# A four-layer hybrid kernel: the image stored once, the first block's sums fetched in two transfers, preparation ahead of the feed-forward

## The chip, the cores and the metric

One Trainium2 chip, one core. The kernel is one launch on that core. The metric is device time in microseconds (us): the time from launch to end of the program as the device measures it, lower is better. It is given as the median of several runs. A separate execution was recorded by the hardware profiler. Engines are named as in the profile: PE is the matrix engine (PEld its weight loads), DVE the vector engine, ACT the scalar (activation) engine, POOL the general engine, SP the engine that issues the transfers (DMA).

## The reference

The input `x` is four images of 128 channels and 64 by 64 pixels, fp32. Each of four layers normalizes and adds to a residual stream. Cut to what matters here:

```python
# layer 0, for each image (x already group-normalized, called xa)
feat = gelu(dwconv3x3(xa, conv1_w) + conv1_b)
ca   = sigmoid(relu(feat.mean((2, 3)) @ ca1_w.T) @ ca2_w.T)
feat = gelu(dwconv3x3(feat * ca, conv2_w) + conv2_b)
sm   = mean over 4x4 patches of 0.7 * sigmoid(head(feat)) + 0.3 * sigmoid(10 * var(xa over channels))
idx  = argsort(-sm)                     # 256 patches; ties keep the lower index first
... the pixels in that order go through a selective scan (Mamba), and back; x += result
x = x + conv3x3(_gn(x)) + bias          # layer 1
# layer 2: t has 4096 tokens of 128 features for each of the 4 images; n = _ln_t(t)
q    = qz_ring(n as 16 heads of 8 + rx_theta)          # queries, keys and values are the same q
attn = softmax(q q^T / sqrt(8));  ctx = attn q         # 4096 x 4096 per head
x1   = ln(n + ctx @ w_comb.T + b_comb) * g1 + beta1    # the first residual
zf   = cos(x1[:8]) * cos(ry_theta)
t    = t + ln(x1 + relu(zf @ w1.T + b1) @ w2.T + b2) * g2 + beta2
t    = t + expert_ffn(ln(t))
# layer 3: linear attention, then another expert_ffn
```

## The kernel before, in words

Data lie channel-major, 128 channels on 128 partitions, and tokens along the free dimension, in chunks of 512 (8 chunks per image, `NCH`).

**Layers 0 and 1** (`layers01`). For each image `in_order(b)` computes the patch order and the reordered tokens, and `scan` runs the selective scan over them. `in_order(0)` runs alone at the start. After that, while image b is scanned, `in_order(b + 1)` is interleaved with it one turn at a time; in the last scan the ends of the images take its place. Inside a scan the order of all five engines is the program's order (a schedule written by hand, SP included): what is issued first runs first on its engine, and a waiting instruction holds those behind it.

In `in_order`, the group-normalized image is filled chunk by chunk into `xp`, padded to 66 by 66. Each depthwise 3x3 convolution runs on PE from a tile `under` of 96 partitions: three row shifts (ky) of 32 channels, for four groups of channels. To build it, `stored(img, i, half)` (L443) writes the image to DRAM three times, once for each ky, with 12 transfers for each half, into `image_d[i]`, and `gather(i, c)` (L453) reads one chunk back with one transfer of 792 KB. Image 0 is `xp`; its first half is stored at the seventh fill and its second after the border of `fp` is set. `first` convolves and its gelu (ACT, L130) writes `fp`, which is image 1, stored in halves once chunks 4 and 7 are there (`first_stored`). After the channel attention, `second` convolves from image 1. A gather is issued three turns ahead of its convolution. `sort` then ranks the 256 patch scores; for the ties it makes a mask `before` (L581) for each half on DVE.

In the scan, for each chunk and group ACT makes `decay` (L907), DVE runs the recurrence `hs` (L911), POOL multiplies by the C factors (L915) and PE sums (`y_ps`).

**Layer 2** (`layer2_attention`), for the blocks b = 0 to 3, one image each: first a transition, in which `prepare(b)` and the tail of the block before, `feed_forward(b - 1)`, run side by side; then `attention(b)`.

- `prepare(b)` has six stages for each of the 8 chunks: fetch, centred, norm, products, running, store. Then it loads the keys and queries of the first head (L1210, 32 transfers) and rounds them on POOL (L1218).
- `attention(b)` goes head by head: PE makes the scores, ACT the exponentials `ex` (L1534), and PE the weighted values: by columns into `ctx` (stored as `num_d` and `den_d`, L1473 and L1474) and, through DVE's 32x32 transposes and the tile `turned_v`, by rows into `acc`. Only half of the symmetric score matrix is computed; the sums of the first quarter of the tokens arrive from both sides, and their second part is stored for each head by L1436 into `around_d`. The values `v` of the next pair of heads are loaded at L1338.
- `feed_forward(b)` has nine stages: fetch, divisors, attended, first_centred, first_norm, cosines, hidden, last_centred, last_norm. Its chunk order is 2 to 7, then 0 and 1. A generator beside it, `firsts`, calls `gathered(c)` for chunks 0 and 1, which need the stored second part: 16 transfers for each chunk (L1582), one for each head, then sums on POOL (L1589, L1594). `divisors` transposes and adds the two halves of the denominators by four products with the constant `pick`, and `rc` (L1610) spreads the reciprocals over the features. `last_norm` adds to x on POOL (L1666) and stores x (L1667).

A transition's generators are run by `run` in round robin, one step of each per round, in the order in which they stand in `parts`. In a transition the engines' order is chosen by a planner which gives priority to what stands earlier in the program; in `attention` it is written by hand for PE, DVE and POOL. The tiles of the transition and those of `attention` use the same memory one after the other, so the first tiles of `attention` wait for the last ones of the transition.

`layernorm_steps` is the normalization with an affine part that is used by both: PE sums the given terms into `ln_xc` (L91; products with `K.center` remove the mean over features, and weights such as `w_comb` are centred once at setup), ACT squares it (`ln_sq`, L107) and copies it (`ln_kept`, L109), PE sums the squares, and DVE and POOL scale (L118 to L126).

**Then** come the experts' layer, layer 3 and the experts' layer again, which the change doesn't touch.

Of the kernel before, what the change touches and what calls it, by code (L numbers as in the profile page):

```python
# [17 lines left out]
P = 128  # L18
NB = 4
HW = 64  # L20
# [10 lines left out]
class Common:  # L31
# [67 lines left out]
    def layernorm_steps(self, out, terms, work, psum, affine=None, bufs=2):  # L99
# [7 lines left out]
        nc.scalar.activation(sq, xc, AF.Square, bias=shift)  # L107
        kept = work.tile([P, CH], F32, name="ln_kept", bufs=bufs)
        nc.scalar.activation(kept, xc, AF.Identity, bias=shift)  # L109
# [160 lines left out]
def layers01(K, xd, dpool, w, w1):  # L270
# [9 lines left out]
    with ExitStack() as ctx:  # L280
# [44 lines left out]
        image_d = [dpool.tile([4, 96, HW * (HW + 2)], F32, name=f"image_d{i}") for i in range(2)]  # L325
# [52 lines left out]
        ones256 = K.ones[:, 0:1].to_broadcast([P, 256])  # L378

# [43 lines left out]
        def in_order(b, made, work, psum):  # L423
# [13 lines left out]
            def stored(img, i, half):  # L437


                n = HW // 2 * (HW + 2)  # L440
                for g in range(4):
                    for ky in range(3):
                        nc.sync.dma_start(  # L443
                            out=image_d[i][g, 32 * ky : 32 * ky + 32, n * half : n * half + n],
                            in_=img[32 * g : 32 * g + 32, HW // 2 * half + ky : HW // 2 * (half + 1) + ky, :].rearrange(
                                "p y x -> p (y x)"
                            ),
                        )

            def gather(i, c):  # L450
                n = 8 * (HW + 2)
                t = unders[c] = work.tile([96, 4, n], F32, name="under", bufs=2)
                nc.sync.dma_start(out=t, in_=image_d[i][:, :, n * c : n * c + n].rearrange("g q f -> q g f"))  # L453
# [31 lines left out]
            for c in range(NCH):  # L485
                fill(c)
                if c == 6:
                    stored(xp, 0, 0)
                yield
# [6 lines left out]
            stored(xp, 0, 1)  # L496

            def first_stored(c):
                if c in (4, 7):
                    stored(fp, 1, c // 5)  # L500
# [66 lines left out]
            def sort():  # L567
# [6 lines left out]
                for h in range(2):  # L574
# [5 lines left out]
                    before = small.tile([P, 256], F32, name="before")  # L580
                    nc.vector.scalar_tensor_tensor(before, K.col, K.row[:, h : h + 1], ones256, ALU.is_gt, ALU.mult)  # L581
                    eq = small.tile([P, 256], F32, name="eq", tag="rank_eq")
                    nc.vector.scalar_tensor_tensor(eq, sm, cl, before, ALU.is_equal, ALU.mult)
# [520 lines left out]
def layer2_attention(K, xd, dpool, w):  # L1104
# [6 lines left out]
    with ExitStack() as ctx:  # L1111
# [48 lines left out]
        pick = cst.tile([2 * NH, NH], F32, name="pick")  # L1160
        nc.vector.tensor_tensor(pick, K.ident[0 : 2 * NH, 0:NH], K.ident[0 : 2 * NH, NH : 2 * NH], ALU.add)
# [22 lines left out]
        around_d = dpool.tile([NH, P, L // NJ // 4], F32, name="around_d")  # L1184
# [135 lines left out]
        def attention(qt, first, dsum, big, two, work, pssc, psctx, psacc):  # L1320
# [83 lines left out]
            def turn():  # L1404
# [28 lines left out]
                if i == 0:  # L1433


                    nc.sync.dma_start(out=around_d[h], in_=accs[h][:, 0].rearrange("p t r -> p (t r)"))  # L1436
# [121 lines left out]
        def feed_forward(b, dsum, work, psum):  # L1558
# [17 lines left out]
            def gathered(c):  # L1576
# [4 lines left out]
                for h in range(NH):  # L1581
                    nc.sync.dma_start(  # L1582
                        out=part[HD * h : HD * h + HD],
                        in_=around_d[h, :, c * P : (c + 1) * P].rearrange("(n d) f -> d n f", d=HD),
                    )
                    if h % 4 == 3:
                        yield
                yield
# [32 lines left out]
            def first_centred(c):  # L1621
# [3 lines left out]
                    x1, [(w_comb, num[:, 0]), (K.center, nrm)], work, psum, (b_comb, g1, beta1), bufs=3  # L1625
# [507 lines left out]
```

## Time and profile before

| what | us |
|---|---|
| median of 3 runs | 10019.67 (10018.24 to 10020.51) |
| the profiled execution | 10014.33, span 10012.5 |
| PE busy | 8755.8 (87%), mean granted clock 0.916 |
| ACT busy | 7414.1 (74%) |
| DVE busy | 7222.2 (72%) |
| POOL busy | 4804.1 (48%) |

| stretch of the span | us |
|---|---|
| front: image 0 alone | 0 to about 280 |
| scans 0, 1, 2 with the next image's order | to about 880, 1480, 2105 |
| scan 3 with the ends of the images | to 2850 |
| `prepare(0)` | 2850 to 2977 |
| attention 0, and the transition after it | 2977.1 to 4258.2, to 4466.6 |
| attention 1, and the transition after it | 4466.6 to 5753.6, to 5962.0 |
| attention 2, and the transition after it | 5962.0 to 7248.8, to 7457.0 |
| attention 3, and the last feed-forward | 7457.0 to 8743.9, to 8887.7 |
| experts, layer 3, experts | 8888 to 10012.5 |

How to read the profile: it is one execution. A row of a table of groups names the line, the engine, the operation, the tile written and the tiles read, the shape, the count, the busy time and the mean duration, and then the idle time of the engine just before these instructions with what ended it. A line can be that of a helper (L91 is the helper that issues the products). A waits line says which instruction stood idle, and for which one it waited. The chain of waits follows back, from the last instruction, what each step was released by. In a table of stretches each engine's busy time is given with its count of instructions, then the granted clock of PE, the mean busy share of the 16 DMA engines and the rate.

### The profile page before, as it was taken

Reading aid. Unit: us, or ns where it says so; the run is one execution under the profiler, and the core shown is the slowest. Engines: PE = TensorE matmul, PEld = TensorE weight load, DVE = VectorE, ACT = ScalarE, POOL = GpSimd, SP = SyncE. Lnnn points to the kernel's source line nnn. Section 1 sums busy time; section 2 is a strip of 40 time slices with the busy share of each in tenths; the row PEclk is TensorE's granted clock in tenths of the full one; section 3 lists DMA queues with packets and bytes.
Section 4 is the critical chain, followed back from the end, with each engine's and each line's share of the span. In section 5 each row is a group of like instructions: output and inputs, shape, how many; then the busy total and the mean of one; then the engine's idle time right before and its main releaser. Section 6 shows DMA issues by size and latency. Waiting matters only on the chain.

```text
span 10012.5 us, 187862 instructions
## 1 busy us (share of the span) xinstructions
PE 8755.8 (87%) x74074; PEld 3353.2 (33%) x74074; DVE 7222.2 (72%) x7883; ACT 7414.1 (74%) x10669; POOL 4804.1 (48%) x3175
## 2 busy tenths in 40 slices
PE   5687888889859999979999979999979999967767
PEld 1122222235433333333333333333333333323433
DVE  1779797998738888848888858888758888743463
ACT  2666766654439999969999969999969999941531
POOL 0567586775525555545555545555545555420000
PEclk9787887889979999989999989999989999978888
DMA  5634536222221211141211141211141111133004
GB/s 127 150 88 101 134 79 152 69 73 81 74 70 37 41 39 39 30 115 38 39 39 39 29 115 39 39 38 39 29 115 39 38 39 39 33 100 118 2 18 152
DMA packets 578291, 669.38 MB, mean 67 GB/s; under 512 B 113592, under 2 KB 369664, under 8 KB 570240
## 3 DMA queue, kind: packets, MB, share of 16 engines
q1 hardware_dynamic: 577408, 657.36, 27.1%
q8 instruction: 584, 9.57, 0.4%
q14 instruction: 299, 2.45, 0.1%
HBM read 446.84 MB, written 143.13 MB: 59 GB/s over the span
## 4 chain that ended last, share of the span: by engine, by line
PE 45%; DVE 4%; DMA 2%; ACT 2%; POOL 1%; issue 1%; SPq 1%; DVEq 0%; POOLq 0%; ACTq 0%
PE ctx_ps L91 20%; PE acc_ps L91 10%; PE score L91 8%; PE ln_xc L91 1%; DMA w<-in_L_ffn_weight 1%; PE ln_var L91 1%; PE hid_ps L91 1%; PE kv L91 1%; PE tok_t L1829 0%; PE ln_var L121 0%; PE pool L91 0%; PE ans_ps L91 0%; DVE ctx L1468 0%; PE o_ps L91 0%; SPq L1210 0%
## 5 line engine op out<-in xcount | busy, mean ns | idle before, releaser
L1534 ACT ACTIVATE ex<-score 128x1024 f32<-128x1024 f32 x5120 | 4927.9, 1037 | 176.0 <-PE score L91 90.2
L91 PE MATMUL ctx_ps<-ex,qt 128*32 128x512 f32 x20480 | 2736.5, 606 | 19.8 <-DVE ctx L1468 19.8
L1483 POOL TENSOR_TENSOR folded<-ex 128x1024 f32<-128x1024 f32 x512 | 1224.2, 2391 | 2124.0 <-ACT ex L1534 1866.1
L1540 DVE STREAM_TRANSPOSE turned<-ex 128x1024 f32<-128x1024 f32 x1536 | 1885.9, 1228 | 351.5 <-ACT ex L1534 279.1
L1516 DVE STREAM_TRANSPOSE turned<-ex 128x1024 f32<-128x1024 f32 x1532 | 1843.0, 1203 | 0.0
L91 PE MATMUL acc_ps<-turned,turned_v 128*32 128x256 f32 x24576 | 1769.4, 379 | 3.0 <-DVE turned L1546 3.0
L911 DVE TENSOR_TENSOR_SCAN hs<-decay,carry,hs 128x512 f32<-128x512 f32 x1024 | 1245.8, 1266 | 248.2 <-ACT decay L907 234.9
L91 PE MATMUL score<-queries,keys 32*128 32x512 f32 x10240 | 1333.6, 497 | 64.4 <-POOL queries L1218 35.8
L91 PEld LDWEIGHTS acc_ps<-turned,turned_v 128*32 128x32 f32 x24576 | 800.8, 110 | 1476.5 <-issue 1327.2
L915 POOL TENSOR_TENSOR hs<-hs,c_sb 128x1024 f32<-128x1024 f32 x512 | 1207.5, 2358 | 108.9 <-DMA c_sb<-c_d 66.5
L907 ACT ACTIVATE decay<-dt,a_neg 128x512 f32<-128x512 f32 x1024 | 693.0, 689 | 662.5 <-DVE hs L911 653.0
L91 PEld LDWEIGHTS score<-queries,keys 32*128 32x128 f32 x10240 | 512.1, 182 | 1160.4 <-ACT ex L1534 801.8
L1346 POOL TENSOR_TENSOR turned_v<-v,quarter 128x1024 f32<-128x1024 f32 x256 | 612.5, 2393 | 266.3 <-PE acc_ps L91 221.8
L91 PE MATMUL y_ps<-hs,pair 128*64 128x512 f32 x2048 | 664.0, 776 | 27.0 <-POOL hs L915 26.9
L1484 POOL TENSOR_TENSOR quarters<-folded 128x512 f32<-128x512 f32 x512 | 658.0, 1285 | 40.1
L91 PEld LDWEIGHTS ctx_ps<-ex,qt 128*32 128x32 f32 x20480 | 406.5, 108 | 655.4 <-issue 599.3
L900 DVE TENSOR_TENSOR hs<-dtx,b_ps 128x2048 f32<-128x2048 f32 x256 | 580.5, 2267 | 55.1 <-PE b_ps L91 29.8
L91 PE MATMUL b_ps<-dbc,state 32*64 32x512 f32 x1024 | 339.6, 745 | 224.5 <-DVE hs L900 224.4
L1534 ACT ACTIVATION_READ_ACCUMULATOR ex<-score 128x1 f32 x2048 | 437.7, 214 | 0.0
L914 POOL COPY carry<-hs 128x2 f32<-128x2 f32 x512 | 98.1, 192 | 700.1 <-DVE hs L911 673.9
L1468 DVE COPY ctx<-ctx_ps 128x512 f32<-128x512 f32 x256 | 176.9, 691 | 329.2 <-PE ctx_ps L91 323.5
L91 PE MATMUL conv<-under,deep 96*32 96x512 f32 x1536 | 217.9, 708 | 136.6 <-DMA under<-image_d 128.3
(371 smaller groups left out, 9156.9 us busy)
## 6 DMA issues: line engine op xcount, KB each, us to landing
c_sb<-c_d SPq DMA_DIRECT2D x512, 128.0 KB
queries<-head_d SPq DMA_DIRECT2D x1024, 64.0 KB
keys<-head_d SPq DMA_DIRECT2D x1024, 64.0 KB
under<-image_d SPq DMA_DIRECT2D x64, 792.0 KB
dt<-dt SPq DMA_DIRECT2D x128, 256.0 KB
dtx<-dtx SPq DMA_DIRECT2D x128, 256.0 KB
v<-value_d SPq DMA_DIRECT2D x1024, 32.0 KB
w<-in_L_ffn_weight SPq DMA_DIRECT2D x32, 1024.0 KB
```

The lines of the kernel that those rows point to most:

```text
L91: self.nc.tensor.matmul(out, lhsT, rhs, start=start, stop=stop)
L900: nc.vector.tensor_tensor(hs, dtx2, bb.unsqueeze(1).to_broadcast([P, NQ, CH]), ALU.mult)
L907: nc.scalar.activation(ex, dt2[:, q, :], AF.Exp, scale=a_neg[:, q, g : g + 1])
L911: nc.vector.tensor_tensor_scan(hs[:, q, :], decays[q - 2 * i], hs[:, q, :], carry[:, g, q : q + 1], ALU.mult, ALU.add)
L915: nc.gpsimd.tensor_tensor(hs[:, two, :], hs[:, two, :], cs.unsqueeze(1).to_broadcast([P, 2, CH]), ALU.mult)
L1346: nc.gpsimd.tensor_tensor(t, v.unsqueeze(2).to_broadcast([P, 4 * BT, 4, HD]), quarter.unsqueeze(1).to_broadcast([P, 4 * BT, 4, HD]), ALU.mult,
L1468: nc.vector.tensor_copy(u, cps)
L1483: nc.gpsimd.tensor_tensor(hs, exs[:, :, 0], exs[:, :, 1], ALU.add)
L1484: nc.gpsimd.tensor_tensor(qs, hs[:, :, 0 : CH // 2], hs[:, :, CH // 2 :], ALU.add)
L1516: nc.vector.transpose(*upright)
L1534: nc.scalar.activation(ex, sps[p], AF.Exp, scale=scale, accum_out=sums[:, t : t + 1] if summed else None)
L1540: nc.vector.transpose(*upright)
```

## The change

It has six parts.

1. The image is stored once, as `image_d[i]` of 128 partitions and 66 by 66 pixels, in four transfers of 16 or 17 rows (`stored(img, i, q)`): for `xp` at fills 3, 5 and 7 and after them, for `fp` after each second chunk. `gather` reads the three row shifts with three transfers.
2. The two masks for ties are made once at setup (`befores`), by another DVE instruction.
3. In `attention`, the sums of heads 0 to 14 are stored in `around_d` with 16 transfers of 8 partitions each, and those of the last head in `around_last_d` with one; `gathered` reads a chunk with two transfers instead of 16, and `firsts` lets 12 turns pass before it begins.
4. In a transition `prepare(b)` stands ahead of `feed_forward(b - 1)` in `parts`, and so issues first in each round.
5. The first residual, n, is added by DVE instead of PE (`more=nrm`): the product of `K.center` and `nrm` goes, ACT's copy becomes a DVE instruction that adds, and ACT squares what DVE wrote.
6. `divisors` turns the denominators with four transposes, and DVE adds the two halves; `pick` goes.

```diff
-    def layernorm_steps(self, out, terms, work, psum, affine=None, bufs=2):
+    def layernorm_steps(self, out, terms, work, psum, affine=None, bufs=2, more=None):
...
-        nc.scalar.activation(sq, xc, AF.Square, bias=shift)
         kept = work.tile([P, CH], F32, name="ln_kept", bufs=bufs)
-        nc.scalar.activation(kept, xc, AF.Identity, bias=shift)
+        if more is not None:
+            nc.vector.scalar_tensor_tensor(kept, xc, shift, more, ALU.add, ALU.add)
+            nc.scalar.activation(sq, kept, AF.Square)
+        else:
+            nc.scalar.activation(sq, xc, AF.Square, bias=shift)
+            nc.scalar.activation(kept, xc, AF.Identity, bias=shift)
...
-        image_d = [dpool.tile([4, 96, HW * (HW + 2)], F32, name=f"image_d{i}") for i in range(2)]
+        image_d = [dpool.tile([P, (HW + 2) * (HW + 2)], F32, name=f"image_d{i}") for i in range(2)]
...
+        befores = [small.tile([P, 256], F32, name=f"before{h}", bufs=1) for h in range(2)]
+        for h in range(2):
+            nc.vector.tensor_scalar(befores[h], K.col, K.row[:, h : h + 1], None, ALU.is_gt)
...
-            def stored(img, i, half):
-                n = HW // 2 * (HW + 2)
-                for g in range(4):
-                    for ky in range(3):
-                        nc.sync.dma_start(
-                            out=image_d[i][g, 32 * ky : 32 * ky + 32, n * half : n * half + n],
-                            in_=img[32 * g : 32 * g + 32, HW // 2 * half + ky : HW // 2 * (half + 1) + ky, :].rearrange(
-                                "p y x -> p (y x)"
-                            ),
-                        )
+            def stored(img, i, q):
+                lo, hi = 16 * q + 1 if q else 0, 16 * q + 17 if q < 3 else HW + 2
+                nc.sync.dma_start(
+                    out=image_d[i][:, lo * (HW + 2) : hi * (HW + 2)], in_=img[:, lo:hi].rearrange("p y x -> p (y x)")
+                )
...
-                nc.sync.dma_start(out=t, in_=image_d[i][:, :, n * c : n * c + n].rearrange("g q f -> q g f"))
+                for ky in range(3):
+                    at = (8 * c + ky) * (HW + 2)
+                    nc.sync.dma_start(
+                        out=t[32 * ky : 32 * ky + 32],
+                        in_=image_d[i][:, at : at + n].rearrange("(g q) f -> q g f", q=32),
+                    )
...
-                if c == 6:
-                    stored(xp, 0, 0)
+                if c in (3, 5, 7):
+                    stored(xp, 0, c // 2 - 1)
...
-            stored(xp, 0, 1)
+            stored(xp, 0, 3)
...
-                if c in (4, 7):
-                    stored(fp, 1, c // 5)
+                if c % 2:
+                    stored(fp, 1, c // 2)
...
-                    before = small.tile([P, 256], F32, name="before")
-                    nc.vector.scalar_tensor_tensor(before, K.col, K.row[:, h : h + 1], ones256, ALU.is_gt, ALU.mult)
                     eq = small.tile([P, 256], F32, name="eq", tag="rank_eq")
-                    nc.vector.scalar_tensor_tensor(eq, sm, cl, before, ALU.is_equal, ALU.mult)
+                    nc.vector.scalar_tensor_tensor(eq, sm, cl, befores[h], ALU.is_equal, ALU.mult)
...
-                    nc.sync.dma_start(out=around_d[h], in_=accs[h][:, 0].rearrange("p t r -> p (t r)"))
+                    sums = accs[h][:, 0].rearrange("p t r -> p (t r)")
+                    if h + 1 < NH:
+                        for k in range(16):
+                            r = slice(HD * k, HD * k + HD)
+                            nc.sync.dma_start(out=around_d[k, HD * h : HD * h + HD], in_=sums[r])
+                    else:
+                        nc.sync.dma_start(out=around_last_d, in_=sums)
...
-                for h in range(NH):
-                    nc.sync.dma_start(
-                        out=part[HD * h : HD * h + HD],
-                        in_=around_d[h, :, c * P : (c + 1) * P].rearrange("(n d) f -> d n f", d=HD),
-                    )
-                    if h % 4 == 3:
-                        yield
-                yield
+                cols = slice(c * P, (c + 1) * P)
+                r = HD * (NH - 1)
+                nc.sync.dma_start(out=part[0:r], in_=around_d[:, 0:r, cols].rearrange("n q f -> q n f"))
+                nc.sync.dma_start(out=part[r:], in_=around_last_d[:, cols].rearrange("(n d) f -> d n f", d=HD))
+                yield from [None] * 4
...
             def firsts():
+                yield from [None] * 12
...
-                tp = psum.tile([P, 4, NH], F32, name="den_t", tag="mm")
+                tp = psum.tile([P, 4, 2 * NH], F32, name="den_t", tag="mm")
                 for j in range(4):
-                    mm(tp[:, j, :], den[:, j * P : (j + 1) * P], pick)
+                    nc.tensor.transpose(tp[:, j, :], den[:, j * P : (j + 1) * P], K.ident[0 : 2 * NH, 0 : 2 * NH])
                 rd = work.tile([P, 4, NH], F32, name="rd")
-                nc.vector.tensor_tensor(rd, tp, dsum[:, 4 * c : 4 * c + 4], ALU.add)
+                nc.vector.tensor_reduce(rd, tp.rearrange("p j (z h) -> p j h z", z=2), AX.X, ALU.add)
+                nc.vector.tensor_tensor(rd, rd, dsum[:, 4 * c : 4 * c + 4], ALU.add)
...
-                    x1, [(w_comb, num[:, 0]), (K.center, nrm)], work, psum, (b_comb, g1, beta1), bufs=3
+                    x1, [(w_comb, num[:, 0])], work, psum, (b_comb, g1, beta1), bufs=3, more=nrm
...
-                    parts = list(feed_forward(b - 1, past, work, psum)) if b > 0 else []
+                    parts = []
                     if b < NB:
                         part, qt, first = prepare(b, big, two, work, psum)
                         parts.append(part)
+                    if b > 0:
+                        parts.extend(feed_forward(b - 1, past, work, psum))
```

More of the change, by code (lines that the diff above doesn't have):

```diff
@@ L1159, in layer2_attention @@
         b_comb, b2 = biases[:, 0:1], biases[:, 1:2]
-        pick = cst.tile([2 * NH, NH], F32, name="pick")
-        nc.vector.tensor_tensor(pick, K.ident[0 : 2 * NH, 0:NH], K.ident[0 : 2 * NH, NH : 2 * NH], ALU.add)
         place = cst.tile([P, 4, 32], F32, name="place")
@@ L1183, in layer2_attention @@
         den_d = dpool.tile([2, NH, L], F32, name="den_d")
-        around_d = dpool.tile([NH, P, L // NJ // 4], F32, name="around_d")
+        around_d = dpool.tile([16, P, L // NJ // 4], F32, name="around_d")
+        around_last_d = dpool.tile([P, L // NJ // 4], F32, name="around_last_d")
         nrm_d = [dpool.tile([P, L], F32, name=f"nrm_d{i}") for i in range(2)]
```

## The prediction

> **What bounds the kernel now.** The page's first part gives no single bound (PE 87% of the span, ACT 74%, DVE 72%), so I cut the time by stage where engine rows change: front (first image alone) 0–280 us; four scans of about 600 us, up to 2850; `prepare(0)` to 2977; four attention blocks of about 1285 us; between them three transitions of 208 us (4258–4467 the first); the last feed-forward 8744–8888. The diff touches the front, three scans (the fourth has no image beside it), the transitions, the last feed-forward, and `attention` by its stores. Then the table of stretches: microseconds, busy PE, PEld, DVE, ACT, POOL with instructions, granted PE clock, DMA share, GB/s.
>
> ```profile
> core 0: us, PE busy (x) PEld busy (x) DVE busy (x) ACT busy (x) POOL busy (x), PEclk, DMA share, GB/s
> 40.00:60.00 20.00, 0.00 (x0) 0.00 (x0) 0.00 (x0) 0.00 (x0) 0.00 (x0) 1.00 0.97 219
> 380.00:620.00 240.00, 192.09 (x777) 50.91 (x779) 163.79 (x129) 161.85 (x208) 138.73 (x100) 0.81 0.64 146
> 620.00:880.00 260.00, 211.18 (x678) 68.79 (x676) 247.44 (x201) 167.89 (x233) 205.73 (x157) 0.82 0.29 71
> 4250.00:4480.00 230.00, 166.01 (x896) 81.94 (x888) 108.07 (x234) 141.30 (x215) 111.64 (x122) 0.79 0.44 116
> 8800.00:8870.00 70.00, 69.15 (x303) 30.04 (x301) 23.95 (x53) 53.64 (x83) 25.41 (x20) 0.96 0.10 34
> ```
>
> In the front every engine stands still while the image is stored. In a scan DVE is the bound in the second half (247 of 260) but not in the first (164 of 240), where the convolutions and their transfers lie. In a transition no engine is full. The last feed-forward is bound by PE.
>
> The waits of 380–620 (engine, line, releaser: total, times, longest), then the image's transfers and `before` (duration ns min/median/max):
>
> ```profile
> DVE hs L911 <- ACT decay L907: 67.3, 21, 18.1
> ...
> PE conv L91 <- DMA under<-image_d: 18.8, 3, 10.7
> ```
> ```profile
> L443 SPq DMA_DIRECT2D image_d<-xp x96: 339/1256/1634, 35.5 to 1585.2; - x96
> ...
> L453 SPq DMA_DIRECT2D under<-image_d x64: 304/311/1332, 63.4 to 1774.4; - x64
> ...
>   PE conv L91: 128.3, 17
> ...
> L581 DVE SCALAR_TENSOR_TENSOR before<-col,row,ones x8: 472/2515/2549, 9.1 to 1834.2; 128x256 f32<-128x256 f32 x8
> ```
>
> An issue takes 1.26 us while stores queue, 0.31 otherwise: SP is held up by them, and the gather behind them is late. PE, ACT and DVE keep the program's order here, so a late gather holds the convolution, the gelu behind it, the `decay` behind that, and DVE's scan.
>
> The end of a transition in the chain of waits (start, us, what):
>
> ```profile
> 4429.69 1.28 POOL x L1666
> 4430.98 0.34 SPq L1667
> 4431.37 0.68 SPq L1210
> ...
> 4465.45 1.03 POOL x L1666
> ...
> 4470.80 2.04 DMA xd<-x
> ```
>
> SP waits for POOL's x before it may load the keys, and the last store lands at 4472.8, after the first score (4466.6).
>
> [...] the 32 `around` loads of a transition occupy 4271.5–4308.3. [...] two chunks of convolution take 5.4 us after a wait and 2.8 without.
>
> **The change part by part.**
>
> *Image stored once, front.* Removed: 24 stores of 264 KB per image (6.3 MB); added: four of 541–574 KB (2.23 MB). At the 219 GB/s of the first stretch 2.23 MB take 10.2 us. Before, stores issue 35.5–62.2 and the first gather lands at 72.3. New: 35.7 + 10.2 + a gather (8.9 us before, 63.4–72.3, as the old stores drain; about 5 on empty queues) = 51: −21. The second image's stores (98.7–111.2) held the seventh gather by 10 us (111.2 for about 101): −10. The second convolution's stall 144.8–148.9 lies behind the half set of 126.6–140.2: −2 taken of its 4. Front: **−33** (−25 to −42).
>
> *Image stored once, scans.* DVE stands still three times per scan; in the first: 9.2 us at 396, behind 24 stores (354.9–386.0); 3.8 at 471; 18.1 at 497–515, behind the second half of fp's stores (480.9–494.6) and a gather issued at 497.2. The scans after it have 8.6, 3.6, 16.9 and 7.9, 2.3, 18.1. Gaps with a convolution but no late gather are 1.9–4.4 us, so I leave 3.5, 2 and 4: −21.5. The gather becomes three issues: 2 × 0.33 us more × 16 = 10 us of SP's time per scan, hidden because each is issued some 13 us ahead; without that cover it would come back in full. `befores`: two of 2.5 us off DVE, **−5** per scan, in full where DVE is 95% busy; the two at setup run beside loads. 3 × 26.5 = 79, of which I take nine tenths because PE and ACT follow closely: **−72** (−45 to −85).
>
> *Transitions.* (a) Sums fetched: 16 loads per chunk become two, of 983 and 64 KB, issued from round 12 on. Before, SP issued x_in at 4273.2 after den, num, nrm and four `around`; it landed at 4281 and ACT stood 22.3 us. Its own latency is 4.2 us in `prepare(0)`. With `prepare` first and `around` later, x_in goes out at about 4269.7 and lands at 4274: −7, and its competitors are gone: −8 taken. On POOL the sums of these chunks (2 × 2.34 + 4 × 1.26 = 9.7 us, from 4302) held `rc` and left PE idle from 4302.3 to 4310.3. All that `firsts` issues moves to rounds 12 to 24: two loads of num and four of sums on SP, past the fetches of six chunks, and six adds on POOL, past the `rc` of as many; POOL is 112 of 230 busy there, and the sums are needed only at chunks 0 and 1, the last two of ff's order. Without this cover the 8 us return in the middle. (b) PE per chunk: the center product L91 ln_xc<-nrm_in is 64 MATMULs of 0.665 us for 32 chunks, 2 each, 1.13 us at the warm 0.55–0.6; `pick` is 256 MATMULs of 0.319 for 32 chunks, 8 each, as timed 2.55 but pipelined and overlapped with their loads, so an estimate of 1.0 in full flow; four one-pass transposes are half the instructions, −0.5 taken (bounds 0 and −1.3). −1.65 × 8 = −13 of PE's 138 us at full clock (warm rows summed: 13.8 for a chunk of ff, 3.5 for one of `prepare`). ACT: kept's Identity −0.68 × 8 = −5.4 of 141. DVE: the new residual reads PSUM at 128x512; the nearest row is L125 SCALAR_TENSOR_TENSOR, 745 ns, and a tensor_reduce of 128x64 about 0.25 (both bounds 0.1–0.5): +1.0 × 8 on an engine 47% busy. It is in the chain, though: ACT's square waits for it, and behind that square, on ACT, whatever the other half of the round issues; +0.75 for each chunk, −0.68 of Identity: about even. (c) With no engine full I take three quarters of PE's gain, −10, and no separate gain for the 8 us of `rc`: **−18** each (−5 to −30), ×3 = **−54**. What is late next: ff's last x, which still sets the first `v`.
>
> *Last feed-forward.* PE is 99% busy, so 8 × 1.65 = **−13** (−8 to −20).
>
> *Attention.* 225 more stores per block on SP, of 8 partitions × 1 KB. Nearest row: the num and den stores, 0.26 + 0.045 us each back to back: 15 × 0.31 = 4.6 us per head of 80, where SP is busy some 36. Queued behind them: `v`, issued 2 us after a head's `around` store (4573.2) and needed at 4591.6; keys, landed 4595.7, needed 4610.9: about 15 us of slack. Cost 0; if an issue took 1.3 us, as image stores do, 15 × 1.3 = 20 exceeds it.
>
> Sum: −33 − 72 − 54 − 13 = **−172**. Profiled before: 10014.3 (span 10012.5), so 9842; the median of the runs lies 5.3 above the profiled one, so **9848**.
>
> **The rivals.** *A, the transitions give nothing:* ff's last x store still comes last (the chain above), and `prepare` ahead each round delays ff a little; for it, PE's 166 of 230 leaves no row full. 9848 + 54 = 9902. *B, the scans keep their stalls:* the gelu's table load and a cold convolution make the gap, not the store (PE's granted clock 0.5 at 471–475 without a store), or three gathers per chunk block SP in turn. `befores` alone stays, 15: 9848 + 57 = 9905. Against it, the three long gaps all begin behind stores. *C, slower:* the small stores in SP's order. If each occupies SP for over 1.0 us (15 us of slack over 15 stores), a head waits; at 1.3 us 5 us × 60 heads = 300, so 9848 + 300 = 10148. For it: 1.26 us at the image stores and 0.65 at L1210's loads; against it: [...] num's stores, of like kind, take 0.26. *D, no effect:* another DMA sets the order; hardly, as the front's 20 idle us are stores alone.
>
> **How the numbers follow.** Forecast 0.60; A 0.18; B 0.13; C 0.05; D 0.02; and 0.02 for a gain beyond 9790. The forecast's own range, from the parts' bounds, half of them turning together, is 9800–9890. To A and B it goes up to 9925, so **9790–9925**, with C and D outside. 0.2% is 20 us, about what a measurement tells from no change. Faster 0.93 (all but C and D), same 0.02, slower 0.05.
>
> **What the profile after should show.** Front: first convolution near 51 us in place of 72.4, no block of SP near 100–111. Scans: image_d stores four per image, DVE's longest gap at the fp stores under 6 us, 600 us falling to about 576. Transitions: x_in landed by 4–5 us after SP's first issue, no `around` before ACT's first square, 208 falling to 190. Last feed-forward 144 to 131. Attention unchanged at 1281–1287; a store's issue at 0.26–0.35 us. It is wrong if attention blocks lengthen (C), if `ln_kept` on DVE becomes what ACT waits for in sum by more than 20 us per transition, or if convolutions still wait for `under<-image_d` by over 60 us in sum (B).

## The result, and the profile after

The changed kernel takes 9897.74 us (median of 4 runs, 9892.74 to 9906.63) against 10020.09 us before. The ratio is 0.9874, with a 95% interval of 0.9857 to 0.9892: 1.3% faster, 122 us of the 172 that were forecast. It lies inside the predicted range and 50 us above the predicted time. The profiled execution took 9895.93 us, its span 9893.6.

Cut into the stages of the table of before, from one profile each (each stage from the first instruction of its kind to the next stage's):

| stage | before | after | difference | forecast |
|---|---|---|---|---|
| front, to the load of the next image | 275.5 | 231.0 | -44.5 | -33 |
| scans 0, 1, 2 | 605.4, 597.2, 625.8 | 586.3, 586.0, 611.4 | -44.7 | -72 |
| scan 3 and `prepare(0)` | 746.0, 127.2 | 747.4, 126.0 | +0.2 | 0 |
| four attention blocks | 1281.2 to 1287.0 | 1280.3 to 1288.5 | +0.5 | 0 |
| three transitions | 208.4, 208.3, 208.2 | 198.9, 200.1, 200.6 | -25.3 | -54 |
| last feed-forward | 143.8 | 134.3 | -9.5 | -13 |
| experts, layer 3, experts | 1124.8 | 1129.0 | +4.2 | 0 |

They sum to the -119 of the spans. The last row's instructions are the same in both kernels; over the profiles of this study it lies between 1125 and 1135, `prepare(0)` between 126 and 134, the front or a scan of the same code varies by up to 7, and the three scans together by up to 11. So a stage of one profile is good to a few microseconds, and where a smaller difference matters below, it is read from three repetitions of a stage or from the timed runs.

The table of stretches after (the same columns as before; the scan's two halves and the transition are the matching ones, shifted by the gain ahead of them):

```profile
40.00:60.00 20.00, 10.69 (x68) 3.17 (x72) 0.00 (x0) 2.84 (x5) 0.00 (x0) 0.94 0.85 196
331.00:571.00 240.00, 201.25 (x842) 54.63 (x842) 184.66 (x146) 176.20 (x231) 151.48 (x114) 0.86 0.52 123
571.00:817.00 246.00, 199.69 (x628) 64.47 (x628) 232.79 (x188) 158.57 (x215) 196.44 (x150) 0.81 0.30 72
4168.50:4367.30 198.80, 139.11 (x736) 65.82 (x732) 115.80 (x241) 121.05 (x186) 97.56 (x114) 0.81 0.48 126
```

In 40 to 60 us, where nothing ran, PE now convolves: the first convolution starts at 46.1 us in place of 72.4. In the scan's first 240 us DVE is busy 185 in place of 164. The transition still has no full engine, and its PE busy time is hardly less than before in proportion (70% of it, 73% before).

The waits of the scan's first half and the image's transfers after:

```profile
DVE hs L916 <- ACT decay L912: 46.3, 21, 7.2
```
```profile
L457 SPq DMA_DIRECT2D under<-image_d x192: 302/430/1965, 39.3 to 1685.7; - x192
L448 SPq DMA_DIRECT2D image_d<-xp x16: 319/506/647, 34.7 to 1496.0; - x16
...
  PE conv L91: 41.4, 11
```

The scan's wait for `decay` falls from 67.3 to 46.3 us and its longest from 18.1 to 7.2. A store's issue takes 0.5 us at the median in place of 1.26, and the convolutions wait 41 us for the image in place of 128. The stand of 18 us behind fp's stores is gone; a gap of 7.2 us, in the place of the first one (9.2 us before), has stayed.

The end of the first transition in the chain of waits after (start, us, what):

```profile
4331.18 1.27 POOL x L1675
4332.48 0.34 SPq L1676
...
4332.86 0.68 SPq L1214
...
4370.15 2.49 POOL x L1675 x2
4372.65 1.96 DMA xd<-x
```

It is the same end as before: x, its store, the key loads behind it on SP, and the last x at the end.

### The profile page after: what moved, and what is told of

Same layout as the page of the kernel before. It is cut to its first block, busy times and chain, and to the rows that moved or that the text cites. A ratio compares the mean times of both kernels' runs of the same rounds, so it can differ in the third digit from the quotient of the medians.

```text
span 9893.6 us, 188260 instructions
## 1 busy us (share of the span) xinstructions
PE 8697.6 (88%) x73882; PEld 3312.7 (33%) x73882; DVE 7277.8 (74%) x7940; ACT 7389.2 (75%) x10637; POOL 4806.0 (49%) x3175
## 4 chain that ended last, share of the span: by engine, by line
PE 69%; DVE 10%; POOL 6%; ACT 5%; DMA 4%; issue 3%; SPq 2%; DVEq 0%; POOLq 0%; ACTq 0%
PE ctx_ps L91 27%; PE acc_ps L91 13%; PE score L91 11%; PE conv L91 4%; POOL hs L920 3%; DVE hs L916 3%; PE y_ps L91 2%; PE xc_ps L91 1%; DVE hs L905 1%; PE ln_xc L91 1%; DMA w<-in_L_ffn_weight 1%; PE ln_var L91 1%; PE b_ps L91 1%; PE hid_ps L91 1%; PE kv L91 1%
## 5 line engine op out<-in xcount | busy, mean ns | idle before, releaser
L1535 DVE TENSOR_REDUCE dacc<-quarters 128x2 f32<-128x512 f32 x508 | 327.1, 644 | 0.0
```

The source lines that it names most:

```text
L1535: nc.vector.tensor_reduce(at, qs, AX.X, ALU.add)
```

## The experiments

Each was run beside the kernel before, on its chip; where two kernels of different chips are compared, their ratios to before are, times 10020 us.

### The image alone

The kernel before with `stored`, `gather`, the new `image_d` and the new places of the stores; the masks `before` stay.

> The kernel before with the image part alone (stored once, three gathers a chunk; the mask `before` still made twice per image). Theory: the image part alone gives nearly the whole gain of the front and the scans, since the mask's 2.5 us are mostly a wait for POOL that passes on to the next DVE instruction: front about 44 us shorter, the three scans together 38 to 43 us shorter, transitions, attention and last feed-forward as before, so about 9935 us. Rival: the masks made once carry their full 5 us per scan, and the scans gain only about 30 here: about 9945 us, the scans each 5 us longer than in the kernel after.

Measured: 9940.79 us, ratio 0.9917 (0.9903 to 0.9932). Front 229.8 us; the scans 582.6, 586.2 and 611.5 us, against 586.3, 586.0 and 611.4 in the kernel after, which has the masks made once. So the masks are worth nothing that these profiles can tell: the three scans take 1780.3 us with them made anew, and 1776.2 to 1783.7 (mean 1779.7) in the seven kernels of this study that have them made once and the same gathers. The forecast had 5 us per scan. Where did the 2.5 us per mask go? In this run:

```profile
L581 DVE SCALAR_TENSOR_TENSOR before<-col,row,ones x8: 473/2517/2548, 9.2 to 1740.9; 128x256 f32<-128x256 f32 x8
L583 DVE SCALAR_TENSOR_TENSOR eq<-sm,cl,before x8: 437/484/1293, 142.8 to 1743.5; 128x256 f32<-128x256 f32 x8
```

and in the kernel after, where the mask is gone:

```profile
L588 DVE SCALAR_TENSOR_TENSOR eq<-sm,cl,before x8: 485/2396/2429, 144.2 to 1745.4; 128x256 f32<-128x256 f32 x8
```

The next instruction took most of the time over: from an `hs` ahead of a mask of scan 0 to one behind it, it is 10.99 and 6.61 us in this run and 10.48 and 6.10 after, so 0.5 us went with each mask, about what the mask takes alone (0.47). The timeline of the kernel after at one of them (start, us, instruction):

```profile
565.45 2.35 POOL L920 TENSOR_TENSOR hs<-hs,c_sb 128x1024 f32<-128x1024 f32 x1
565.68 2.40 DVE L588 SCALAR_TENSOR_TENSOR eq<-sm,cl,before 128x256 f32<-128x256 f32 x1
```

DVE's instruction ends at 568.08, 0.28 us after POOL's (567.80). In the front, where POOL is idle, the same instruction takes 0.48. The same holds at all six places in the scans, in the kernel before (`before`, 2.51 to 2.55 us) and in the kernel after (`eq`, 2.40 to 2.43): DVE's instruction ends 0.28 us after the `hs` product of POOL that runs beside it. So the 2.5 us were not the mask's work, which took 0.47 in the front: by these times DVE stood until POOL was done, and the row shows the stand as busy time. Why it stands is not shown.

### The order of the two generators

The kernel after with the feed-forward first again:

```diff
-                    parts = []
+                    parts = list(feed_forward(b - 1, past, work, psum)) if b > 0 else []
                     if b < NB:
                         part, qt, first = prepare(b, big, two, work, psum)
                         parts.append(part)
-                    if b > 0:
-                        parts.extend(feed_forward(b - 1, past, work, psum))
```

> The kernel after with `feed_forward` ahead of `prepare` again. Theory S: prepare ahead gives 8 us at the start of a transition, since x_in leaves first, but in the middle SP, which issues in order, stands at the store of the normalized block with the feed-forward's loads queued behind it, and gives some of it back. Feed-forward first then loses at the start only the three issues ahead of x_in (about 2 to 4 us, as the `around` loads are gone) and wins in the middle: a transition of 192 to 199 us (after: 199 to 201), the whole 0 to 20 us faster than the kernel after. Rival O: the order is what gives the gain: each transition goes back to 205 to 208 us, the whole 15 to 25 us slower than after.

Measured: 9867.43 us (9863.23 to 9873.24), ratio 0.9843 (0.9826 to 0.9859): some 30 us faster than the kernel after. The transitions are 190.5, 187.2 and 189.1 us, 11 us shorter each, more than Theory S had. So the order is not a gain; it costs 11 us in each transition. In the first, x_in (the fetch of `prepare`) leaves at 12.8 us after the last score in place of 11.4, and `prepare`'s first product starts at 17.3 in place of 14.7 (22.8 before): with the sums' loads gone from the start, under 3 of the 8 us that are won there are the order's.

The order alone, on the kernel before:

> The kernel before with `prepare` ahead of `feed_forward` and nothing else changed. Theory P (what is second on every engine is delayed, and the feed-forward's end is what the transition waits for): x_in leaves at 11.5 us in place of 14.9 and the first square of `prepare` comes up to 8 us sooner, but the transition is not shorter, 208 to 220 us in place of 208: the whole within 5 us of before or up to 35 us slower. Rival, the prediction's step (a): the start's gain stays, 199 to 203 us: the whole 15 to 27 us faster than before.

Measured: 10049.89 us (10031.84 to 10061.8), ratio 1.0016 (1.0008 to 1.0023). The transitions are 214.4, 215.1 and 215.4 us, 6.7 longer each. `prepare`'s first product starts at 14.8 us in place of 22.8, so here the order alone wins all 8 us at the start, and loses them and more later: it makes the kernel slower.

Is it SP that stands at a store with loads behind it? The kernel after with the normalized block's store moved from `norm` to `products`:

```diff
             def norm(c):
                 next(halves.pop(c), None)
-                nc.sync.dma_start(out=nrm_d[b % 2][:, c * CH : (c + 1) * CH], in_=nrms[c])
 
             def products(c):
+                nc.sync.dma_start(out=nrm_d[b % 2][:, c * CH : (c + 1) * CH], in_=nrms[c])
```

> The kernel after (prepare ahead) with the store of the normalized block, at which SP stands up to 14.6 us, issued one stage later, with `products`. Theory S: SP's stand at that store, with the feed-forward's loads queued behind it, is what prepare ahead costs: a transition falls from 200 to 188 to 194 us, the whole 18 to 35 us faster than after, near the kernel with feed-forward first. Rival P: the order on PE, ACT and DVE costs it, since the feed-forward, whose last store ends the transition, comes second on every engine: a transition stays at 197 to 202 us, the whole within 8 us of after.

Measured: 9898.53 us, ratio 0.9876 (0.9860 to 0.9893), no different from after; transitions of 197.0, 197.6 and 196.6 us, 3 us shorter each, as rival P had it. SP's waits in the first transition, after and then in this run:

```profile
SPq L1247 <- DVE nrm L127: 38.4, 7, 9.6
SPq L1304 <- POOL part L1303: 25.3, 8, 7.5
...
SPq L1247 <- DVE rd L1616: 14.6, 1, 14.6
```
```profile
SPq L1304 <- POOL part L1303: 55.5, 8, 17.0
...
SPq L1249 <- DVE nrm L127: 10.0, 2, 5.8
```

The stand at the normalized block (53 us in sum) is nearly gone, but SP then stands at the next store of `prepare` (25 to 55 us). So the move didn't free SP. That the stand at this store is not the order's cost follows from the run with the feed-forward first, where SP stands at the same store nearly as long (46 us in sum), and the transition is 8 us shorter:

```profile
SPq L1247 <- DVE nrm L127: 30.9, 5, 11.0
...
SPq L1247 <- DVE rd L1615: 15.0, 1, 15.0
```

### The first fetch ahead

With the feed-forward first, the late store and the paired gather of the next heading together, the kernel is the fastest of the study:

> The kernel after with feed-forward first, the normalized block's store one stage later and the second gather issued with the first. If the three add up: transitions of 182 to 187 us (feed-forward first 187 to 191, and 3 to 5 for the store), scans as with the paired gather: 15 to 30 us faster than feed-forward first alone, so 9838 to 9853 us. If the late store takes from the same wait as the order did: transitions of 187 to 191 us and about 9855 to 9865 us.

Measured: 9853.56 us (9850.32 to 9857.24), ratio 0.9828 (0.9814 to 0.9843), against 9898.53 and 9884.13 for the late store and the paired gather alone on the same chip. The transitions are 189.7, 188.8 and 186.8 us: the late store adds nothing to the order. To this kernel, one step of `prepare` ahead of the rounds:

```diff
+                    if 0 < b < NB:
+                        next(part)
                     run(*parts)
```

> The same kernel (feed-forward first, late store, paired gather, 9853.6 us), with the first fetch of `prepare` alone issued ahead of the feed-forward's three loads. If the start gates what follows, each transition is 1 to 3 us shorter: 9844 to 9850 us. Otherwise within 3 us of 9853.6.

Measured: 9883.61 us (9881.36 to 9892.14), ratio 0.9852 (0.9838 to 0.9867), 24 us slower; transitions of 196.7, 198.8 and 198.1 us, 9.4 longer each. The expectation overlooked what this does: after it, the steps come p0 f0 p1 f1 and so on, which is exactly the order with `prepare` ahead. So this is a second test of the order, on another kernel, with the same answer, and it shows how little the order is: `prepare` one step earlier against the feed-forward.

What lengthens? ACT's waits in the first transition with the feed-forward first, then in the kernel after:

```profile
ACT ln_sq L112 <- PE ln_xc L91: 16.1, 9, 5.7
ACT phi L244 <- DVE phi L243: 9.6, 5, 3.0
```
```profile
ACT phi L244 <- DVE phi L243: 17.7, 4, 5.3
...
ACT ln_sq L112 <- PE ln_xc L91: 9.2, 5, 3.1
...
ACT ln_kept L113 <- POOL x L130: 5.6, 1, 5.6
```

The same row in the fastest kernel, and with the first fetch ahead:

```profile
ACT phi L244 <- DVE phi L243: 8.6, 5, 3.0
```
```profile
ACT phi L244 <- DVE phi L243: 16.6, 4, 5.3
```

Over the three transitions ACT's wait at `phi` (the cosine of `prepare`, whose argument DVE makes) grows from 28.8 to 53.1 us in the first pair and from 25.5 to 49.8 in the second, 8 us for each transition. One step earlier, `prepare`'s cosine stands on ACT ahead of its argument, with the feed-forward's work behind it. That is the pattern in both pairs. It isn't settled as the cause. ACT's wait at `ln_kept` grows nearly as much (1.1 to 24.1 and 2.8 to 22.5), and that at the square of L112 falls by 25 and 30. That all of ACT's waits together grow by 32 and 27 us, as much as the transitions lengthen (33 and 28), says little, since an engine with the same work in a longer stretch stands longer; POOL's grow by some 30 too. And on the kernel before, where the order costs 6.7, the wait at `phi` falls (32.1 to 9.2) and PE's at `ln_var` grows (79.6 to 117.6).

Where in a transition the time goes can be read from the feed-forward's chunks, by the first ACT instruction of their `cosines`, counted from the last score (mean of the three transitions). With the feed-forward first and then in the kernel after, the third chunk comes at 92 and 94 us and the fifth at 140 and 152. In the second pair these are 90 and 94, then 140 and 150; on the kernel before and with the order alone 107 and 108, then 156 and 165. So in all three pairs most of the loss comes between the feed-forward's third chunk and its fifth, and 0 to 3 us before it. What is shown is the cost of the order and its place; which engine passes it on depends on what else is in the transition, and stays open.

### The first gap of a scan

SP's longest wait where the first convolution of scan 0 begins, in the kernel after:

```profile
SPq L808 <- POOL carry L919: 18.9, 1, 18.9
```

The second chunk's gather is issued behind it, at 353.0, and its convolution starts at 360.0, a moment before DVE runs dry (360.8). The convolution of 5 us (its MATMULs take 1.06 us at a granted clock of 0.52 in 360 to 365, where warm ones take 0.59), the gelu and a table load of 1.28 us follow, before `decay` can go on: DVE stands 7.2 us. The edit issues the first two gathers together:

```diff
+            def early(c):
+                for k in {0: (0, 1), 1: ()}.get(c, (c,)):
+                    gather(0, k)
...
-            yield from staged(NCH, 2, lambda c: gather(0, c), None, None, first, None, first_stored)
+            yield from staged(NCH, 2, early, None, None, first, None, first_stored)
```

> The kernel after with the second chunk's gather of the first convolution issued together with the first chunk's. Theory: the gap of 5.5 to 7.2 us that VectorE keeps at the start of the first convolution in each scan comes from that gather, which stands behind SP's 18.8 us wait at the dt load; it then leaves before this wait, and each of the three scans is 2 to 4 us shorter, the front unchanged or 1 to 3 us shorter: the whole 5 to 13 us faster than after. Rival: the gap is PE's half clock and ACT's table loads; the scans move by less than 1.5 us each.

Measured: 9884.13 us (9867.63 to 9892.88), ratio 0.9857 (0.9842 to 0.9872), some 17 us faster than after, with overlapping intervals. The scans are 579.0, 582.6 and 604.7 us. One profile's scans vary by as much as the gain, so here are all: the three scans take 1765.5 to 1770.0 us in the four kernels with the paired gather and 1776.2 to 1783.7 in the seven without, so 13 us less in the mean, where 6 to 12 were expected. The wait in the first half, after and then here:

```profile
DVE hs L916 <- ACT decay L912: 46.3, 21, 7.2
```
```profile
DVE hs L920 <- ACT decay L916: 40.2, 21, 4.4
```

The gap at the first convolution is 2.5 us in this scan and 3.7 and 4.2 in the next two, where it was 7.2, 5.5 and 7.1. So most of what had remained was a late gather, behind a wait that the stores had covered.

### The first residual, the divisors

The residual by PE again (`[(w_comb, num[:, 0]), (K.center, nrm)]`, no `more`):

> The kernel after with the first residual added by PE again (two more products of 0.6 us a chunk, ACT's copy in place of DVE's addition). Theory: the transitions follow a chain of waits, not PE's sum, so each transition moves by less than 3 us either way; the last feed-forward, where PE was 99% busy, is longer by 8 x 1.1 = 9 us; the whole about 5 to 15 us slower than after. Rival of the prediction's step: PE's time counts in the transitions too, each 7 to 9 us longer, the whole 30 to 36 us slower.

Measured: 9908.48 us (9907.26 to 9912.55), ratio 0.9886 (0.9871 to 0.9901), 12 us slower than after by the ratios, whose intervals overlap. The transitions are 205.0, 202.3 and 204.5 us, 4.1 longer each, between the theory and its rival. (The runs with the paired gather and with the small stores four times over, which have the transitions' code of after, show 199.2 to 203.4; against all nine transitions it is 3.2.) The last feed-forward is 135.4 in place of 134.3, so 1 us where 9 were expected: up to its third chunk it is 2 us shorter, and in the rest, where PE is nearly full, 3 longer. The divisors by products with `pick` again:

> The kernel after with the divisors made by the four products with the constant again, and no reduction on DVE. Theory: a transition moves by less than 2 us either way and the last feed-forward by less than 2 us, since neither follows PE's sum: the whole within 6 us of after. Rival of the prediction's step: 0.5 us of PE a chunk counts, 3 to 4 us in each transition and 4 in the last feed-forward: the whole 13 to 16 us slower.

Measured: 9899.21 us, ratio 0.9875 (0.9860 to 0.9889), the same as after. The transitions are 199.1, 202.2 and 195.8, no longer than after. The last feed-forward is 138.6, 4.3 longer, and outside the 133.6 to 135.4 of the eight kernels that have the new divisors and the new fetch of the sums. So the rival's 4 us came there, where the theory had less than 2. In the transitions and in the timed runs the divisors are worth nothing that shows.

### The sums, and the 12 turns

The kernel after with one store a head, and the 16 loads a chunk from the first round on:

> The kernel after with the first block's sums stored and fetched as before (one store a head, 16 loads a chunk from the first round on). Theory: the 32 loads come back at the start of a transition, behind x_in now, and take SP and the DMA queues for some 37 us: a transition of 203 to 208 us, the last feed-forward 2 to 5 us longer, the attention blocks unchanged within 1 us (the 225 extra stores cost nothing): the whole 15 to 30 us slower than after. Rival: with prepare ahead the loads lie beside other work and a transition stays at 199 to 201 us: the whole within 5 us of after.

Measured: 9931.93 us (9926.10 to 9934.49), ratio 0.9908 (0.9893 to 0.9922), 34 us slower than after by the ratios, more than the theory had. The transitions are 209.9, 208.1 and 210.8 us, 9.7 longer each, and the last feed-forward 143.8, 9.5 longer; attention is the same within 1 us in each block. In the first transition x_in leaves as in the kernel after, but the second and third fetch of `prepare` leave 9 and 15 us later, behind the loads. Next, the fastest kernel without the 12 empty turns:

> The kernel with feed-forward first, late store and paired gather (9853.6 us, transitions of 187 to 190), without the 12 turns that `firsts` waits. Theory: the gain of the new fetch is that 4 us of issues replace 37 us of them, so two loads a chunk at once cost little: transitions of 187 to 194 us, the whole up to 15 us slower or the same. Rival: the gain is that the sums' 2 MB and POOL's additions keep away from the start: transitions of 195 to 203 us, the whole 20 to 40 us slower.

Measured: 9879.15 us (9870.21 to 9891.85), ratio 0.9847 (0.9833 to 0.9862), 19 us slower by the ratios. The transitions are 192.8, 194.6 and 196.6 us, 6.2 longer each, and the last feed-forward is 140.1 (5.5 longer). So the delay counts for much, with two loads a chunk as well, and both expectations were half right. That it counts for more than the number of loads is likely but not shown, since the 9.7 was measured with `prepare` ahead and the 6.2 with the feed-forward first.

### The small stores, four times over

```diff
                         for k in range(16):
                             r = slice(HD * k, HD * k + HD)
-                            nc.sync.dma_start(out=around_d[k, HD * h : HD * h + HD], in_=sums[r])
+                            for _ in range(4):
+                                nc.sync.dma_start(out=around_d[k, HD * h : HD * h + HD], in_=sums[r])
```

> The kernel after with each of the 240 small stores of a block issued four times over (the same data to the same place): 45 + 15 more issues per head, 60 x 0.31 = 19 us of SP in place of 5. The prediction put the slack of SP's order at about 15 us per head. If that reading is right, heads wait some 4 us each: an attention block 40 to 70 us longer, the whole 160 to 280 us slower than after. Rival: the slack is larger, since the loads behind the stores are made a whole head ahead: attention blocks within 3 us of 1280 to 1288, and 16 small stores a head are hidden with room to spare.

Measured: 10078.34 us (10037.45 to 10099.34), ratio 1.0043 (1.0019 to 1.0066), some 169 us slower than after by the ratios. The attention blocks are 1311.9, 1336.1, 1334.3 and 1323.5 us, 32 to 48 longer each. So 5 us of SP per head are hidden and 19 are not. What holds the block up is not what the prediction named. The waits of DVE, PE and POOL in 1000 us of attention 1:

```profile
DVE ctx L1479 <- DMA den_d<-ctx: 46.2, 9, 7.9
```
```profile
PE ctx_ps L91 <- DVE ctx L1479: 39.2, 22, 6.2
```
```profile
POOL queries L1222 <- DMA num_d<-ctx: 29.4, 6, 7.5
POOL queries L1222 <- DMA queries<-head_d: 16.8, 3, 7.8
...
POOL keys L1222 <- DMA keys<-head_d: 6.0, 5, 2.3
```

In the kernel after, DVE's wait and POOL's aren't among those of that stretch, and PE's is 4.3 us:

```profile
PE ctx_ps L91 <- DVE ctx L1478: 4.3, 13, 0.3
```

The stores of num and den, queued behind the small ones, hold the buffers of `ctx`, and PE waits for these: 35 us more, of the 48 by which the block lengthens (over the four blocks 23 to 36 of 32 to 48). The queries and keys of the next head are late too, as POOL's waits show, but no wait of PE for them is among those of the stretch; `v` was late once there, by 1.9 us. A small store's issue takes 0.29 us at the median in both kernels.

## Why the prediction was right or wrong

**The whole: in the range, for reasons that are in part luck.** 9898 us lies above the 9800 to 9890 of the forecast's own parts, in the stretch that was left for rival A (9902) and rival B (9905). Neither took place: the transitions gave 25 of 54 us and the scans 45 of 72. The front gave 11 us too much, and the order of the two generators, forecast as part of a gain, took some 30 us back.

**Image stored once, front: right, too small.** -44.5 for -33. The first convolution starts at 46.1, where 51 was worked out. The sum let the first gather wait until all four stores had landed; this gather left at 39.3, 0.4 us after the issue of the last (38.9). From there to the last gelu of the first convolution it takes 39.4 us in place of 54.0 (-14.6, forecast -10), and the second convolution gives 5 (forecast 2); 1.4 of it is lost after. The gather took 6.8 us from issue to the first product, where about 5 was the author's estimate; in the kernel before, the gathers issued at 77.8 and 88.1, with no store just ahead, took 5.8 and 5.7. (The old stores move 6.5 MB per image, not 6.3; nothing rests on it.)

**Image stored once, scans: mechanism right, two terms mis-sized.** The forecast was -24 each, the measurement -19.1, -11.2 and -14.4. The gap of 17 to 18 us went as forecast, to 3.5 to 4.9. The sum took the first scan's three gaps for all: by the nine gaps that it lists, less 9.5 a scan, it is 20.0 and not 21.5 each, which makes -68 in place of -72. The step "I leave 3.5" for the first gap failed, as 5.5 to 7.2 us stayed: the stores were blamed for all of it, while another wait of SP, 18.9 us at the dt load, stood ahead of the same gather. The paired gather shows this. Rival B was right in so far as that gap holds a cold convolution (1.06 us a MATMUL) and a table load (1.28), but an earlier gather takes them out of DVE's way. The step "`befores`, in full where DVE is 95% busy" failed nearly wholly: about 1 us per scan on DVE's own row for 5, and nothing that the scans show, since the row's 2.5 us held a wait for POOL that the next instruction inherits (`eq`, 2.40 us). A minimum of 472 ns beside a median of 2515 in the same row, of one shape, was the sign of it in the profile before. Also, waits of `hs` for `b_ps` grew by 2 to 5 us per scan.

**Transitions: less than half, wrong sharing, and a sign.** -8.4 each for -18. The forecast of 190 us is what the kernel takes with feed-forward first (187 to 191), by luck, since other shares make it up; the change as made takes 199 to 201. The step that failed is (a), which carries the 8 us won at the start through to the end ("With `prepare` first and `around` later, x_in goes out at about 4269.7"). The start went as worked out: x_in leaves 11.4 us after the last score and the first product starts at 14.7 in place of 22.8. But the order alone wins these 8 us as well and lengthens the transition by 6.7, and on the kernel after it costs 11. Rival A named this ("`prepare` ahead each round delays ff a little") and put it too low to be the likeliest. The sums' fetch by itself is worth 9.7. PE's share in (b) and (c) was about twice too large: the residual gives 3 to 4 where three quarters of 9 were taken, the divisors nothing. DVE's new instructions took what was put: 0.74 us for the residual (0.745) and 0.28 for the reduction (about 0.25, the author's estimate). These parts don't add up to -8.4 (9.7 and 4 less 11 is under 3), so what one of them is worth depends on the others.

**Last feed-forward: right size, wrong sharing.** -9.5 for -13. Up to its third chunk it is 5.7 us shorter: there ACT's first square waited 26.7 us, last for a load of the sums, and waits 19.5 after. The rest, where PE was full in 8800 to 8870, is 3.8 shorter. Taken back one at a time, the residual is worth 1 us (9 forecast), the divisors 4.3 (4 forecast) and the sums' fetch 9.5 (nothing forecast here); they overlap.

**Attention: right.** +0.5 us over four blocks with 240 small stores each. The threshold of rival C is real, between 5 and 19 us of SP per head (at 19 a block takes 32 to 48 us more); what carries it is mainly the buffers of `ctx`, not `v` or the keys.

## What to carry to other kernels

A busy row with a minimum far below its median, for one shape (0.47 beside 2.52 us here), can hold a wait: look at what the other engines run beside it, since removing such an instruction may only hand the wait to the next. Where two generators share engines that run in order, a shift of one by a single step can cost more than the earlier load gains (here the first product came 8 us sooner and the transition was 6.7 longer), so measure the order apart from what it is bundled with. And a gap that begins behind a slow transfer can have a second wait under it (here 18.9 us of SP at the dt load): look at all that the issuing engine does between the last useful transfer and the late one.

## What the runs showed of the hardware

A DVE scalar_tensor_tensor of 128x256 (`before`, `eq`), 0.47 to 0.49 us in the front, where POOL is idle, took 2.40 to 2.55 us beside a POOL tensor_tensor of 2.34 to 2.36, and ended 0.28 us after it. A transfer of 983 KB that replaced 15 of 64 KB was issued in 0.35 to 1.5 us; the one of 64 KB right behind it held SP for 0.33 to 8.3 us, 3.2 at the median.
